# Two meetings of sequences in an attention and LoRA kernel: turns, router and value stores placed one or two products later, one scaling ahead of a score round

## The chip, the cores and the metric

The kernel runs on one core of a Trainium2 chip. The metric is the device time of one execution in microseconds (us). The time before is the median of three runs; a profile of one further execution is read beside it.

## The reference

Four sequences of 1024 rows with 1024 columns, all in float32. With x of shape (4, 1024, 1024):

```python
x = x + attn(layernorm(x), wq, wk, wv, wo)      # 32 heads of 32, rotary q and k, causal softmax
n = layernorm(x)
logits = n @ route_w.T                          # 8 experts
gate = one_hot(argmax(logits)) * max(logits)    # top 1
h = n @ A                                       # 8 experts x 16 hidden values
x = x + ((gate * h) @ Bw)
```

The layer norms have no weights. All weights of the attention are 1024 x 1024; the last step is a LoRA adapter of rank 16 for each of the 8 experts.

## The kernel before, in words

**Units and slots.** The kernel goes through 32 units: 4 sequences (b) of 8 head groups (g), each of 4 heads. Unit u has b = u // 8 and g = u % 8. A unit is a list of eleven slots (`SLOTS`). Nine are score rounds (`score_round`): the scores of one to four of the sixteen 64-row tiles go to PSUM, ScalarE (ACT) copies them to SBUF (L441), GpSimd (POOL) adds the causal mask on the diagonal (L444), VectorE (DVE) finds the row maxima, here called tops (L462, L483), ACT exponentiates in place (L491), and DVE turns the probabilities (L516). The two others, "second" and "first", apply the values (`apply`, L632): "second" those of the upper half of the unit before, "first" those of the lower half of this unit.

**What fills the slots.** Beside each unit stands a list of steps, `between[u]`: the q, k and v products of the next unit (`chain`, L337; eight 128x512 products for each of six chains), and from the second sequence on the end of the layer for one row tile of the sequence before (`finish_steps`): sixteen products of `wo` (`project`, L749, called `p` in the change; the first eight give the first half of the columns), then the tail: `turn` (transposes, L201, tensors pt_f), `route` (L771, ph), `turn_hidden` (L800, pw) and `adapt` (L810, pf, with the additions at L813 and the store of y at L814). The loop at the end of the function takes so many of these steps after each round. So the order of the instructions is written out by this Python code; each engine then works through its own list in order and waits on semaphores.

**The meeting of two sequences.** In the last unit of a sequence (g = 7) the products of the next unit need the next sequence, normalized and turned. `Norm` has these steps for each of eight row tiles of 128 rows: `load` (a DMA), `find` (mean and variance on DVE, L178 to L182, and the root on POOL, L184), `scale` (L189 on DVE), `turn` (eight transposes on TensorE, L201, tensors pt_a, then two copies by ACT to xnT, L203 and L205; then the next load). `change_steps` puts them in order among the last v chain of the present sequence (`h`, eight products held back for this), the wo products `p`, the tail, and the new chains. The first meeting (into b = 1) takes another branch. The second (u = 15) and the third (u = 23) take the branch `if p`, which the change rewrites. The lists `h`, `p` and `chains` are indexed in it, and the Python order in it is TensorE's order; a score round of the unit falls between two of its steps wherever the slot ends.

**Buffers.** A pool `ps` of four PSUM banks serves products, transposes and the tail; a new user waits until the engine that empties the old one is done. Chunks of wo, of the router weights (in_ra) and of the adapter (in_bw) go through four SBUF buffers (`take_chunk`, `load_chunk`): the load of chunk n + 4 is issued behind the product that used chunk n. In a meeting, tiles 3 and 6 of the new sequence lie in the next unit's qT, tile 4 in its kT.

**SyncE's queue.** All DMAs are issued by SyncE (SP), in the program's order. `stores` holds what is to be put to DRAM: the attention result of "second" (L665) and the unit's values (L531, four DMAs); they are issued in the loop at a slot given by `r`. The values are read back in another layout by eight DMAs (`loads`, L537), which `scatter` mixes into the steps to come, two apart. `second` is the index 2 in `SLOTS`; index 3 is the round of tiles 2, 1, 0 and 9, index 4 that of tile 15, index 5 that of tile 14.

Of the kernel before, what the change touches and what calls it, by code (L numbers as in the profile page):

```python
# [57 lines left out]
def weave(main, other):  # L58

    if not other:  # L60
        return list(main)
    out, taken = [], 0
    for n, step in enumerate(main):
        out.append(step)
        due = (n + 1) * len(other) // len(main)
        out += other[taken:due]
        taken = due
    return out + list(other[taken:])
# [3 lines left out]
def tile_preln_attn_then_top1_lora(  # L72
# [18 lines left out]
    B, S, D = x.shape  # L91
# [5 lines left out]
    NG = HEADS // HG  # L97
# [77 lines left out]
    def find_moments(src, name):  # L175
        stats = small.tile([P, D // 512, nc.vector.BN_STATS_DIM], F32, tag="stats", name=f"st_{name}")
        for i in range(D // 512):
            nc.vector.bn_stats(stats[:, i, :], src[:, i * 512 : (i + 1) * 512])  # L178
        mv = small.tile([P, nc.vector.BN_AGGR_DIM], F32, tag="mv", name=f"mv_{name}", bufs=3)
        nc.vector.bn_aggr(mv, stats)  # L180
        ve = small.tile([P, 1], F32, tag="ve", name=f"ve_{name}")
        nc.vector.tensor_scalar(ve, mv[:, 1:2], EPS, None, ALU.add)  # L182
        rstd = small.tile([P, 1], F32, tag="rstd", name=f"rstd_{name}", bufs=3)
        nc.gpsimd.tensor_tensor(rstd, ve, half_sb, ALU.pow)  # L184
        return mv, rstd
# [43 lines left out]
    def do_postponed(cost):  # L229
        for item in list(postponed):  # L230
            item[0] -= cost
            if item[0] <= 0:
                postponed.remove(item)
                item[1]()
# [12 lines left out]
    class Norm:  # L247
# [32 lines left out]
        def find(self, t):  # L280
            while self.found <= t and self.found in self.x:
                k = self.found
                self.moments[k] = find_moments(self.x[k], f"a{self.b}_{k}")
                self.found += 1
# [26 lines left out]
        def scaling(self, t):  # L311
            return Step(lambda: self.scale(t), 0.0)

        def turning(self, t):
            return Step(lambda: self.turn(t), 2.0 if self.b == 0 else 1.3)
# [169 lines left out]
    def release_exps():  # L485
        to_exp.extend(next_exp)
        next_exp.clear()
# [187 lines left out]
    def load_wo():  # L675

        for n in range(2):
            cols = slice(n * 512, (n + 1) * 512)
            wt = big.tile([P, NC, 512], F32, tag="xnT", name=f"wo_{n}", bufs=2)
            wo_all.append(wt)  # L680
            for c in range(NC):
                nc.sync.dma_start(wt[:, c, :], wo[c * P : (c + 1) * P, cols])
# [3 lines left out]
    def load_adapter():  # L686

        ra_all = NC * (E + ER)
        room = big.tile([P, ra_all + D + TB * D], F32, tag="prob0", name="adapter")
        kept["ra"] = room[:, :ra_all].rearrange("p (c n) -> p c n", n=E + ER)  # L690
        kept["bw"] = room[:ER, ra_all : ra_all + D]
        for k in range(TB):
            kept[k] = room[:, ra_all + D + k * D : ra_all + D + (k + 1) * D]
        nc.sync.dma_start(kept["ra"], ra.rearrange("(c p) n -> p c n", p=P))
        nc.sync.dma_start(kept["bw"], bw)
# [152 lines left out]
    def change_steps(u, norm, project, tail, held):  # L848

        p, h, turning, scaling = project, held, norm.turning, norm.scaling
        out, chains = [], []
        for n, tb in (("q", 0), ("k", 0), ("q", 1), ("k", 1), ("v", 0), ("v", 1)):
            chains += chain(u, n, tb)
        if p:
            turn, route, turn_hidden, adapt = tail
            find = norm.finding
            load_last = Step(lambda: norm.load(7), 0.0)
            out += [*h[:2], turn, *h[2:4], find(3), p[0], h[4], turning(2), h[5], p[1], route, scaling(3)]  # L860
            out += [find(4), h[6], p[2], h[7], p[3], turn_hidden, scaling(4), *p[4:6], adapt, load_last]
            out += [p[6], find(5), p[7], turning(3), scaling(5), *p[8:10], turning(4), *p[10:12]]
            chains = weave(chains[:-6], p[12:]) + chains[-6:]
            out += [*chains[:2], find(6), *chains[2:4], scaling(6), turning(5), *chains[4:6], find(7)]
            out += [*chains[6:8], scaling(7), turning(6), *chains[8:14], turning(7)]
            return out + chains[14:]
        for t, n in zip(range(TB, NT), (3, 4, 4, 4)):
            out += [*chains[:n], turning(t)]
            del chains[:n]
        return out + chains  # L870
# [149 lines left out]
    def do(s):  # L1020
        if s.chunk:
            s.run(numbers[s])
        else:
            s.run()
        do_postponed(s.cost)
# [40 lines left out]
    def scatter(steps, apart):  # L1066

        for k, s in enumerate(steps):
            todo.insert(min(len(todo), 1 + apart * k), s)

    n_slots = len(SLOTS)
    second, first_ = SLOTS.index("second"), SLOTS.index("first")
    final = len(units) - 1
    for u, (b, g) in enumerate(units):
        do_postponed(math.inf)
        do_postponed(math.inf)
        todo.extend(between[u])
        ends_at = n_slots
        if b + 1 < B and g + 1 == NG:
            if b:  # L1080
                norms[b + 1].load(3, 4)
        if u == final:
            load_wo()
            ends_at = second
        for r, pieces in enumerate(SLOTS):
            if pieces == "second":
                release_exps()
            if pieces == "second":
                if u == final:
                    todo.extend(early)  # L1090
                    ends_at = second + 3
                put, loads = spread_values(u)

                def meanwhile():
                    nc.vector.transpose(vTs[u], vTs[u])
                    if u in ahead_of:
                        ahead_of[u][0]()

                if u:
                    apply(u - 1, 1, meanwhile)  # L1100
                else:
                    meanwhile()
                stores.append(put)
            elif pieces == "first":
                apply(u, 0)
                find_tops(u)
                ended.clear()
            else:
                release_exps()
                turn_probabilities()  # L1110
                if second < r < first_:
                    join_sums(u, 0)
                if r == second + 1 and u in ahead_of:
                    ahead_of[u][1]()
                score_round(u, pieces)
                if r == second - 1 and u:
                    while any((u - 1, t) in places for t in range(QT, 2 * QT)):
                        exponentiate_some(1)
                        turn_probabilities()
                    join_sums(u - 1, 1)  # L1120
                if r != first_ - 1:
                    find_tops(u)
                exponentiate_some(SHARE / 3)
                next_exp.extend((u, t, h) for t in ended for h in range(HG))
                if r != first_ - 1:
                    ended.clear()
                if r in (second + 1, first_ + 1):
                    for put in stores:
                        put()
                    stores.clear()  # L1130
                    if u == final and r == first_ + 1:
                        load_adapter()
                if r == second + 2:
                    scatter(loads, 2)
                    if u in late_fetch:
                        do(late_fetch[u])
                        for k in range(3 if b == 1 else 0):
                            load_chunk(k)
            if u == final:
                if r == second + 3:  # L1140
                    todo.extend(parts)
                    ends_at = first_ + 2
                if r == first_ + 1:
                    todo.extend(wholes)
                    ends_at = n_slots + 2
            held_back = APART_BY if r < second else 0
            ahead = LENGTHS if not b and u + 1 < NG else [1.0] * ends_at
            fill(
                ahead[r] / sum(ahead[r:ends_at]),
                held_back,  # L1150
                0.0 if pieces in ("first", "second") else SHARE * 2 / 3,
            )
# [61 lines left out]
```

## Time and profile before

| | |
|---|---|
| median of 3 runs | 2727.84 us (2725.76 to 2735.31) |
| profiled execution | 2729.0 us, its span 2727.2 us |
| granted TensorE clock, mean | 0.995 |
| TensorE (PE) busy | 2671.2 us, 98% |
| VectorE (DVE) busy | 2141.2 us, 79% |
| ScalarE (ACT) busy | 1725.2 us, 63% |
| GpSimd (POOL) busy | 604.4 us, 22% |
| second meeting, about | 1150 to 1250 us from the span's start |
| third meeting, about | 1820 to 1920 us |

PEld is TensorE's load of the stationary operand, which overlaps its products. A wait is written as the waiting engine, tile and line, an arrow, and the engine, tile and line that ended it; then the total in us, how often, and the longest. A row of the timeline has the start, the duration, the engine, the line, the operation, the tile written and those read, and in brackets the idle time ahead of it. A float32 product stands as x2 in the timeline. Times are from the start of the span.

### The profile page before, as it was taken

To read this page: it belongs to the slowest core of one execution; us is meant where nothing else is said; L and a number is where in the kernel's file an instruction comes from. 1 tells how busy PE (TensorE), PEld (TensorE's weight loads), DVE (VectorE), ACT (ScalarE), POOL (GpSimd) and SP (SyncE) were. 2 spreads that over 40 slices of the span, in tenths; PEclk is the share of its full clock that TensorE was granted. 3 is DMA by queue.
4 is the path that set the end of the run, shared out by engine and by line. 5 is a ranking of instruction groups with operands and counts; after the bars stand their busy time and mean duration, and the time that the engine had idled before them with its cause. 6 is when DMAs were issued, how large, how long until landed. Compare 5 with 4: busy or idle time off the path is not lost.

```text
span 2727.2 us, 84063 instructions
## 1 busy us (share of the span) xinstructions
PE 2671.2 (98%) x35116; PEld 1305.0 (48%) x35116; DVE 2141.2 (79%) x4254; ACT 1725.2 (63%) x4980; POOL 604.4 (22%) x847
## 2 busy tenths in 40 slices
PE   8999999999999999989999999999999999999998
PEld 5444444444444544445444444444544444544445
DVE  4899999887777787887777878888778777777555
ACT  2878777876665676655666666766567666666421
POOL 2222222222221222222222222222212222222000
PEclk9999999999999999999999999999999999999999
DMA  3223233226555445652654444465354554446421
GB/s 118 60 72 74 75 77 84 53 56 174 139 140 131 126 131 155 167 157 61 163 161 134 135 131 132 136 187 142 83 159 135 159 136 133 131 132 185 123 69 53
DMA packets 465259, 332.19 MB, mean 122 GB/s; under 512 B 160496, under 2 KB 381936, under 8 KB 464880
## 3 DMA queue, kind: packets, MB, share of 16 engines
q1 hardware_dynamic: 464880, 326.83, 43.7%
q8 instruction: 276, 4.52, 0.7%
q14 instruction: 103, 0.84, 0.1%
HBM read 276.48 MB, written 50.24 MB: 120 GB/s over the span
## 4 chain that ended last, share of the span: by engine, by line
PE 79%; DVE 13%; ACT 3%; DMA 2%; POOL 1%; issue 1%; SPq 0%; POOLq 0%; DVEq 0%; ACTq 0%
PE po L749 15%; PE pq L337 14%; PE pk L337 13%; PE pv L337 11%; PE s L430 11%; PE av L632 8%; DVE top L462 4%; DVE pr L516 3%; PE ph L771 2%; PE pf L810 2%; ACT pr L491 1%; ACT pr L441 1%; DVE both L483 1%; PE pt_f L201 1%; DMA chunk<-in_wo 1%
## 5 line engine op out<-in xcount | busy, mean ns | idle before, releaser
L491 ACT ACTIVATE pr<-pr,both 128x256 f32<-128x256 f32 (+15 forms) x2048 | 1044.5, 519 | 55.5 <-DVE both L483 55.5
L441 ACT COPY pr<-s 128x640 f32<-128x640 f32 (+14 forms) x544 | 525.3, 1017 | 668.6 <-PE s L430 668.0
L462 DVE TENSOR_REDUCE top<-pr 128x2 f32<-128x960 f32 (+15 forms) x768 | 650.6, 893 | 256.8 <-POOL pr L444 256.2
L516 DVE STREAM_TRANSPOSE pr<-pr 128x1024 f32<-128x1024 f32 (+11 forms) x768 | 664.5, 907 | 33.7 <-ACT pr L491 30.4
L444 POOL TENSOR_TENSOR pr<-pr,causal_sb 128x128 f32<-128x128 f32 x512 | 239.0, 473 | 1152.2 <-ACT pr L441 1143.9
L337 PE MATMUL pv<-xnT,wv 128*128 128x512 f32 x1024 | 486.2, 602 | 0.0
L337 PE MATMUL pq<-xnT,wq 128*128 128x512 f32 x1008 | 479.1, 603 | 0.2 <-ACT xnT L203 0.2
L337 PE MATMUL pk<-xnT,wk 128*128 128x512 f32 x1008 | 476.8, 602 | 0.0
L430 PE MATMUL s<-kT,qT 32*32 32x256 f32 (+4 forms) x17408 | 393.8, 385 | 8.7 <-POOL pr L444 3.3
L491 ACT ACTIVATION_READ_ACCUMULATOR pr<-pr,both 128x1 f32 x2048 | 401.3, 196 | 0.0
L749 PE MATMUL po<-chunk,attn 128*128 128x512 f32 x736 | 379.7, 601 | 4.8 <-DMA chunk<-in_wo 4.8
L430 PEld LDWEIGHTS s<-kT,qT 32*32 32x32 f32 x17408 | 187.5, 103 | 266.2 <-issue 100.8
L337 PEld LDWEIGHTS pk<-xnT,wk 128*128 128x128 f32 x1008 | 181.2, 190 | 234.8 <-issue 234.5
L337 PEld LDWEIGHTS pq<-xnT,wq 128*128 128x128 f32 x1008 | 183.8, 192 | 226.1 <-issue 224.2
L337 PEld LDWEIGHTS pv<-xnT,wv 128*128 128x128 f32 x1024 | 185.6, 190 | 218.0 <-issue 217.2
L632 PE MATMUL av<-pr,vals 64*32 64x256 f32 (+3 forms) x12288 | 273.6, 321 | 6.9 <-DVE pr L516 6.5
L632 PEld LDWEIGHTS av<-pr,vals 64*32 64x32 f32 x12288 | 214.9, 106 | 115.5 <-issue 69.8
L483 DVE TENSOR_TENSOR both<-top 32x4 f32<-32x4 f32 (+3 forms) x1152 | 206.6, 179 | 23.8
L749 PEld LDWEIGHTS po<-chunk,attn 128*128 128x128 f32 x736 | 135.2, 190 | 170.1 <-issue 147.5
L652 DVE TENSOR_TENSOR at<-av,by 128x256 f32<-128x256 f32 x128 | 48.1, 417 | 110.0 <-PE av L632 71.5
L749 PE MATMUL po<-wo,attn 128*128 128x512 f32 x256 | 119.1, 607 | 2.3 <-DMA attn<-attn 2.3
L370 POOL TENSOR_TENSOR qT<-rawq,cos_sb 128x512 f32<-128x512 f32 x64 | 82.1, 1283 | 143.0 <-ACT rawq L363 143.0
(89 smaller groups left out, 1565.9 us busy)
## 6 DMA issues: line engine op xcount, KB each, us to landing
chunk<-in_wo SPq DMA_DIRECT2D x368, 256.0 KB, 3.8
vals<-vd SPq DMA_DIRECT2D x256, 128.0 KB, 4.3
x<-in_x SPq DMA_DIRECT2D x56, 512.0 KB, 5.0
wq<-in_wq SPq DMA_DIRECT2D x32, 512.0 KB, 4.7
wk<-in_wk SPq DMA_DIRECT2D x32, 512.0 KB, 3.9
wv<-in_wv SPq DMA_DIRECT2D x32, 512.0 KB, 4.2
vd<-vT SPq DMA_DIRECT2D x128, 128.0 KB, 4.5
out_y<-x SPq DMA_DIRECT2D x32, 512.0 KB, 2.6
```

Source lines behind the costliest of these rows:

```text
L337: nc.tensor.matmul(at["p"], lhsT=wt[:, c, :], rhs=xnTs[b, tb][:, c, :], start=(c == 0), stop=(c == NC - 1),)
L370: nc.gpsimd.tensor_tensor(dst[:, cols], raw, cos_sb[:, cols], ALU.mult)
L430: nc.tensor.matmul(sc[i * SQ : (i + 1) * SQ, h, at : at + w].rearrange("p (j k) -> p j k", k=SQ), lhsT=of_q[rows, 2 * t + half], rhs=of_k[ ...
L441: nc.scalar.copy(pr[:, :, k0 : k0 + w], sc[:, :, at : at + w])
L444: nc.gpsimd.tensor_tensor(diagonal, diagonal, causal_sb.unsqueeze(1).to_broadcast([P, HG, SQ]), ALU.add)
L462: nc.vector.tensor_reduce(top[:, k, h : h + step], places[u, t][:, h : h + step, :], AX.X, ALU.max, negate=True,)
L483: nc.vector.tensor_tensor(dst[rows], src[rows], src[other], op)
L491: nc.scalar.activation(pr[:, h, :], pr[:, h, :], AF.Exp, bias=tops[u, t][:, h : h + 1], accum_out=dens[u, t // QT][:, t % QT, h : h + 1],)
L516: nc.vector.transpose(pr, pr)
L632: nc.tensor.matmul(avs[half][h * HD : (h + 1) * HD, t0:, :], lhsT=v[rows, j, h * HD : (h + 1) * HD], rhs=rhs, start=(j == 0), stop=(j == n ...
L749: nc.tensor.matmul(st["po"], lhsT=lhsT, rhs=rhs, start=(c == start), stop=(c == stop))
L771: nc.tensor.matmul(ph, lhsT=st["ynT"][:, c, :], rhs=w[:, c - i * RA, :], start=(c == 0), stop=(c == NC - 1),)
```

## The change

Three things change, for the second and third meeting alone.

1. In `change_steps` tile 2's turn, the router, tile 3's turn and tile 4's turn stand one or two products later among the v products `h` and the wo products `p`; `p[3]` and `p[4]` both stand ahead of `turn_hidden`.
2. Tile 6 (the seventh) is scaled one chain product earlier, which puts it ahead of the score round that falls there; its turn stays where it was.
3. In the loop, the stores of the attention result and of the values are issued one slot later (after the round of tile 15 in place of that of tile 2), and the loads of the values are scattered one slot later too.

```diff
-            out += [*h[:2], turn, *h[2:4], find(3), p[0], h[4], turning(2), h[5], p[1], route, scaling(3)]
-            out += [find(4), h[6], p[2], h[7], p[3], turn_hidden, scaling(4), *p[4:6], adapt, load_last]
-            out += [p[6], find(5), p[7], turning(3), scaling(5), *p[8:10], turning(4), *p[10:12]]
+            out += [*h[:2], turn, *h[2:4], find(3), p[0], h[4], p[1], h[5], turning(2), h[6], p[2], route]
+            out += [scaling(3), find(4), h[7], p[3], p[4], turn_hidden, scaling(4), p[5], adapt, load_last]
+            out += [p[6], find(5), p[7], p[8], turning(3), scaling(5), p[9], p[10], turning(4), p[11]]
             chains = weave(chains[:-6], p[12:]) + chains[-6:]
-            out += [*chains[:2], find(6), *chains[2:4], scaling(6), turning(5), *chains[4:6], find(7)]
-            out += [*chains[6:8], scaling(7), turning(6), *chains[8:14], turning(7)]
+            out += [*chains[:2], find(6), chains[2], scaling(6), chains[3], turning(5), *chains[4:6]]
+            out += [find(7), *chains[6:8], scaling(7), turning(6), *chains[8:14], turning(7)]
             return out + chains[14:]
...
-                if r in (second + 1, first_ + 1):
+
+                meet = b and b + 1 < B and g + 1 == NG
+                if r in (second + (2 if meet else 1), first_ + 1):
                     for put in stores:
                         put()
                     stores.clear()
                     if u == final and r == first_ + 1:
                         load_adapter()
+                if r == second + (3 if meet else 2):
+                    scatter(loads, 2)
                 if r == second + 2:
-                    scatter(loads, 2)
                     if u in late_fetch:
                         do(late_fetch[u])
```

## The prediction

> **What bounds the kernel now.** I read the page first: TensorE (PE) is busy for 98% of the span, so only time in which PE waits, or runs at a lowered clock, can be won back.
>
> ```profile
> span 2727.2 us, 84063 instructions
> PE 2671.2 (98%) x35116; PEld 1305.0 (48%) x35116; DVE 2141.2 (79%) x4254; ACT 1725.2 (63%) x4980; POOL 604.4 (22%) x847
> ```
>
> The busy time by stage shows where. Columns: stretch, its length, PE, PEld, DVE, ACT and POOL busy, granted clock, DMA share, GB/s.
>
> ```profile
> 1150.00:1250.00 100.00, 92.11 (x1129) 46.19 (x1133) 79.33 (x161) 59.98 (x169) 23.57 (x34) 0.98 0.48 137
> 1250.00:1820.00 570.00, 569.51 (x7597) 274.19 (x7596) 451.53 (x900) 368.79 (x1073) 127.13 (x176) 1.00 0.51 139
> 1820.00:1920.00 100.00, 92.95 (x1193) 47.52 (x1184) 81.82 (x163) 61.63 (x171) 23.62 (x34) 1.00 0.50 141
> 1920.00:2500.00 580.00, 580.00 (x7706) 279.02 (x7689) 458.05 (x909) 372.49 (x1082) 129.11 (x177) 1.00 0.49 135
> ```
>
> The two changed meetings idle PE for 7.9 and 7.1 us. Between and after them PE is full, so what a meeting gains or loses reaches the end one to one. The waits of PE in the second meeting:
>
> ```profile
> PE po L749 <- DMA chunk<-in_wo: 2.3, 2, 1.3
> PE pt_a L201 <- DVE qT L189: 2.3, 1, 2.3
> PE pt_a L201 <- ACT yn L203: 2.1, 1, 2.1
> PE pt_a L201 <- ACT xnT L203: 0.7, 1, 0.7
> PE pw L800 <- DVE wh L790: 0.5, 1, 0.5
> ```
>
> They are, in time: tile 2's turn (2.12), the turned hidden row (0.51), tile 3's turn (0.68), two chunks of wo (1.31 and 0.98), tile 6's turn (2.26). The third meeting repeats them 672.4 us later, with one chunk wait of 1.47. Each has a row of the change aimed at it. The question is what is late next.
>
> **First clue: VectorE (DVE).** From 1147 to 1196 it is busy 46.57 of 49 us, in both meetings, and the chain of waits runs along it from 1140 to 1183 almost without a break.
>
> ```profile
> 1147.00:1196.00 49.00, 45.66 (x767) 25.18 (x782) 46.57 (x94) 30.84 (x87) 9.27 (x16) 1.00 0.53 161
> ```
>
> The order of the built kernels shows DVE's own order unchanged up to tile 6's scaling. POOL's order does not change at all. So PE can run ahead there, but its next wait on DVE comes at the same time as before.
>
> **Part 1, tile 2's turn and the router.** PE's new order after the product at 1165.34 is: product of wo, scores of tile 5, v product, turn, v product, wo, router (ph), v product, values (av). With the old steps (0.86 a product, 0.95 before scores, 1.57 for these scores, 0.96 after them, 0.93 a turn) the turn comes at 1169.7, behind ACT's two copies of yn (ended 1168.92): the 2.12 is gone. But the router's bank is the one the turn filled, and ACT must empty it.
>
> ```profile
> 1168.33 0.59 ACT L205 COPY yn<-pt_f 128x512 f32<-128x512 f32 x1
> 1170.43 0.58 ACT L203 COPY xnT<-pt_a 128x512 f32<-128x512 f32 x1
> 1171.37 1.89 ACT L441 COPY pr<-s 128x768 f32<-128x768 f32 x3
> ```
>
> On ACT that copy now stands behind the scores' copies (1.75), two exponentials of 288 (1.05) and two of 256 (1.0): 1170.43 + 3.8 + 0.57 = 1174.8. PE arrives at 1172.5, so a new wait of 2.34 takes the old one's place. Router 1.86 and product 0.96 lead to av at 1177.65; av needs DVE's four transposes of probabilities, ended 1177.75 before and not earlier now. Before, av started at 1177.77. Gain: 0.1.
>
> **Part 2, the hidden row.** One more product stands ahead of pw, so wh (DVE, 1182.97) is waited for no longer: gain 0.5, and with smaller steps the second half of av starts at 1184.24 instead of 1185.01.
>
> **Part 3, tile 3's turn.** The first product of the second half of wo moves ahead of it, and now takes the bank of the spread sums. The turn gets the banks of pf, which DVE empties with the two additions at L813 (ended 1193.18). DVE had one gap here, 0.35 for ACT's copy of the sums, which comes 0.77 earlier: so 1192.83. The chunk of the moved product is issued after pf and took 2.9 to land: PE waits 0.45 for it and twice, 0.3 and 0.6, for L813. Scores of tile 2 start at 1194.37 instead of 1194.80: gain 0.43.
>
> **Part 4, tile 4's turn and the chunks.** SP's queue (start, length):
>
> ```profile
> 1193.21 0.34 SPq L814 DMA_DIRECT2D out_y<-x  x1
> 1193.61 0.42 SPq L126 DMA_DIRECT2D x<-in_x  x1
> 1194.14 1.27 SPq L706 DMA_DIRECT2D chunk<-in_wo x2
> ```
>
> The two awaited chunks stand behind the store of y, which waits for L813. They move by L813's 0.35 only: landing near 1198.69 instead of 1199.04, the second near 1200.8. The attention and value stores, moved a slot on, stood behind them already; in 1197 to 1201 only 62 packets were under 512 B. Taking them away gives between nothing and 0.9 (the attention store's 256 KB at the 281 GB/s of 1195 to 1205); I take nothing, as the landings follow the order of issue. One of the chunks is now wanted ahead of tile 4's turn, which covered 0.93 of its landing: PE arrives at 1196.28 and waits 2.41 (2.55 in the third meeting, where the landing was 0.16 later), then turns, then takes the second chunk, which has landed by then. In the third meeting this order alone loses 0.6, as its second chunk was never late.
>
> **The clock.** Idle PE costs a second time:
>
> ```profile
> 1197.00:1207.00 10.00, 7.71 (x19) 3.25 (x17) 5.59 (x14) 4.30 (x14) 2.29 (x5) 0.83 0.90 246
> 2556.00:2566.00 10.00, 7.67 (x34) 3.15 (x14) 4.87 (x13) 4.90 (x16) 0.45 (x1) 0.83 0.96 211
> 1210.00:1220.00 10.00, 7.74 (x54) 3.37 (x53) 8.03 (x15) 8.09 (x28) 2.25 (x3) 1.00 0.47 96
> ```
>
> 0.83 over 10 us is 1.7 us lost (8 products at 1203.01 took 4.25 against 3.60). In PE's timeline single waits of 2.33, 2.40, 2.60, 2.70 and 3.91 were all followed by it, one of 2.23 was, and those of 2.12, 2.13, 2.26 and 2.27 were not; the two chunk waits, 2.29 together, were. The Trainium skill ("TensorE: Matmul & The Clock Gate", on how the gate oscillates in real kernels) asks only that PE not idle for over some 3.4 us. By that rule no new wait here lowers the clock, and the second meeting even sheds its 1.7. By the rows, 2.41 and 2.55 both lower it. I take the rows: second meeting 1.7 as before, third meeting 1.7 new. The router's 2.34 is at the edge; I take it as not.
>
> **Part 5, tile 6 scaled ahead of a round.** DVE was idle for 6.2 us ahead of the tops of tile 15, and the scaling stood behind them. The tile's load now stands behind one more chunk and lands about 0.5 later (1203); with 1.65 of statistics, 0.55 on POOL and 0.8 the scaling ends near 1206.2, before the turn's 1212.2 and before the tops are due (1209.5). The 2.26 goes. Next late is ACT: the first k product needs the bank of rawq, whose copy ends 7.07 after the start of the scores of tile 15, 0.6 after PE arrives.
>
> **Part 6, stores and loads of values.** The attention and value stores (7.85 of SP's time before) stand behind the last two wo chunks. Six of eight value loads now also stand behind a router chunk, whose buffer comes free at about 1217. They land near 1217.5 + 2.9 + 4.1 = 1224.5; av of this unit starts near 1237. Cost nothing, with 12 us of cover.
>
> **The sum.** Second meeting: scores of tile 15 start at 1198.69 + 0.86 (chunk) + 0.93 (turn) + 0.86 (chunk) + 3.57 (four q products) + 1.7 (clock) = 1206.6; first k product at 1206.6 + 7.07 = 1213.7, before 1215.95: gain 2.25. Third, in the second's times: 1206.8, and 1213.87 against 1213.46: loss 0.4. Together 1.85. The profiled execution took 2729.0 (2727.2 and 1.8 around the span), so 2727.15; the median of the runs is 1.16 lower: 2726.0.
>
> **Rivals.**
> - *No new half clock* (the skill's rule): for it, the nearest wait of 2.27 passed at full clock; against it, five of five from 2.33 on. The gains are then 3.7 and 1.3: 2722.8. Chance 0.25.
> - *The router's wait lowers the clock too*: av, the sums and L813 come later, by 1.1 net a meeting: 2728.2 for both. It shares 0.65 with my forecast.
> - *The waits vanish as aimed at*: 7.9 + 7.1 + 1.7 = 16.6, so 2711. Against it: DVE's full 49 us. Chance 0.03.
> - *Slower: the values come late.* SP's queue is in order, and six value loads now wait behind a chunk's release. Each microsecond by which they land after av is due shows once in each meeting. It decides from 1237, 12.5 us later than I reckon; 0.5% slower (13.6 us) needs 1245.5, giving 2743. For it, the stores took 8.0 to land in a crowded queue; against it, the queue is empty by then. Chance 0.05.
>
> About 0.5% is what a measurement of this kernel can tell from no change; nothing but the last two passes it, and 0.02 is left for what I overlook. Range 2721 to 2731: 1.8 below the second case and 2.8 above the third, for the scatter of runs (2725.8 to 2735.3). Chances: faster 0.03, same 0.91, slower 0.06.
>
> **What would show it.** Right: PE's waits list ph behind ACT xnT (2.3, twice), po behind a chunk (2.4 to 2.6, twice), pt_a behind DVE x (under 1), and none on yn or qT; half-clock stretches in both meetings near 1199 and 1871. Wrong: a chunk wait under 1.5 (the landing moved with PE), av before 1177, or any wait of av on vals.

## The result, and the profile after

| | before | after |
|---|---|---|
| median of 17 runs, us | 2729.38 (2724.47 to 2737.35) | 2724.51 (2720.74 to 2729.37) |
| ratio, 95% interval | | 0.9984 [0.9977, 0.9991] |

The change makes the kernel 4.9 us faster by the medians, 2.5 to 6.3 by the interval. That is less than 0.5% and more than the 1.85 us of the forecast; the median lies inside its range, between the forecast (2726.0) and the rival without new half clock (2722.8). The profiled execution after took 2727.9 (its span 2726.1), more than the median of its runs, so its span alone tells little. First lines of its page:

```profile
span 2726.1 us, 84061 instructions
PE 2670.2 (98%) x35116; PEld 1305.3 (48%) x35116; DVE 2141.5 (79%) x4254; ACT 1725.0 (63%) x4980; POOL 602.5 (22%) x847
```

Nothing there shows a gain of 0.2%. The busy time by stage, after (stretch, length, PE, PEld, DVE, ACT, POOL busy, granted clock, DMA share, GB/s):

```profile
1150.00:1250.00 100.00, 94.53 (x1195) 48.58 (x1184) 81.53 (x163) 61.68 (x171) 23.36 (x34) 0.98 0.49 142
1250.00:1820.00 570.00, 568.27 (x7563) 273.52 (x7547) 450.29 (x898) 367.20 (x1070) 126.76 (x176) 1.00 0.51 139
1820.00:1920.00 100.00, 94.87 (x1155) 48.06 (x1154) 80.58 (x159) 63.30 (x173) 23.27 (x34) 0.97 0.48 138
1920.00:2500.00 580.00, 580.00 (x7677) 279.07 (x7676) 458.85 (x910) 371.57 (x1080) 128.85 (x178) 1.00 0.49 136
```

The meetings now idle TensorE for 5.5 and 5.1 us, where it was 7.9 and 7.1. But the clock of the third fell to 0.97: a busier TensorE there is partly a slower one. Its waits, in the second meeting and then in the third:

```profile
PE po L749 <- DMA chunk<-in_wo: 2.5, 1, 2.5
PE ph L771 <- ACT xnT L203: 2.1, 1, 2.1
PE pk L337 <- ACT rawq L363: 0.6, 1, 0.6
```

```profile
PE po L749 <- DMA chunk<-in_wo: 2.5, 2, 2.3
PE ph L771 <- ACT xnT L203: 2.0, 1, 2.0
PE pk L337 <- ACT rawq L363: 0.6, 1, 0.6
```

The waits on yn, on wh, on xnT ahead of tile 3 and on tile 6's qT, at which the change aimed, are gone. Two of the three in their place are as long as the old ones: the router's and the chunk's. TensorE's timeline has them with their times; first two rows of the second meeting, then two of the third:

```profile
1176.85 3.58 PE L771 MATMUL ph<-chunk,yn 128*128 128x136 f32 x16 [2.07 <-ACT xnT L203]
...
1202.01 1.12 PE L749 MATMUL po<-chunk,attn 128*128 128x512 f32 x2 [2.49 <-DMA chunk<-in_wo]
```

```profile
1848.33 2.67 PE L771 MATMUL ph<-chunk,yn 128*128 128x136 f32 x16 [1.99 <-ACT xnT L203]
...
1873.21 1.69 PE L749 MATMUL po<-chunk,attn 128*128 128x512 f32 x2 [2.27 <-DMA chunk<-in_wo]
```

A router of 3.58 us, against 2.02 before, and a pair of products of 1.69 against 1.12 ran at half clock, wholly or in part; the pair behind 2.49, the longest wait, did not. This contradicts any rule by the length of the wait alone.

To compare meetings I take the stretch from the start of the turn of yn (pt_f) to the start of the first k product, the same instructions in both kernels:

| | second meeting | third meeting |
|---|---|---|
| before | 54.06, one half clock | 51.57, none |
| after | 51.50, one half clock | 52.44, two half clocks |

At a full 1.7 us for each half clock (at most that: part of it can lie beside a wait), the waits themselves gave 2.6 us in the second meeting and up to 2.5 us in the third.

### The profile page after: what moved, and what is told of

Read it like the earlier page. It is cut to its first block, busy times and chain, and to the rows that moved or that the text cites. A ratio compares the mean times of both kernels' runs of the same rounds, so it can differ in the third digit from the quotient of the medians.

```text
span 2726.1 us, 84061 instructions
## 1 busy us (share of the span) xinstructions
PE 2670.2 (98%) x35116; PEld 1305.3 (48%) x35116; DVE 2141.5 (79%) x4254; ACT 1725.0 (63%) x4980; POOL 602.5 (22%) x847
## 4 chain that ended last, share of the span: by engine, by line
PE 79%; DVE 12%; ACT 3%; DMA 2%; issue 1%; POOL 1%; SPq 1%; POOLq 0%; DVEq 0%; ACTq 0%
PE po L749 14%; PE pq L337 14%; PE pk L337 13%; PE pv L337 12%; PE s L430 11%; PE av L632 9%; DVE top L462 3%; DVE pr L516 3%; PE ph L771 2%; PE pf L810 2%; ACT pr L491 2%; DMA chunk<-in_wo 1%; ACT pr L441 1%; DVE both L483 1%; PE pt_f L201 1%
## 5 line engine op out<-in xcount | busy, mean ns | idle before, releaser
L652 DVE TENSOR_TENSOR at<-av,by 128x256 f32<-128x256 f32 x128 | 48.2, 418 | 112.0 <-PE av L632 72.8
```

## The experiments

Each kernel was timed in five rounds beside the kernel before on the same chip, whose median was 2728.2, 2727.9 and 2728.6 us in the three groups (e1 to e4, e5 to e8, e9 to e12). Ratios are to that kernel, each with its 95% interval. There were 16, 13, 21 and 21 runs of e1 to e4, 5, 10, 13 and 5 of e5 to e8, and 22, 22, 6 and 6 of e9 to e12: e5, e8, e11 and e12 are the least sure.

### The scaling of tile 6 alone (e1), and everything but it (e2)

e1 against the kernel before; e2 is the kernel after with these two lines as before.

```diff
-            out += [*chains[:2], find(6), *chains[2:4], scaling(6), turning(5), *chains[4:6], find(7)]
-            out += [*chains[6:8], scaling(7), turning(6), *chains[8:14], turning(7)]
+            out += [*chains[:2], find(6), chains[2], scaling(6), chains[3], turning(5), *chains[4:6]]
+            out += [find(7), *chains[6:8], scaling(7), turning(6), *chains[8:14], turning(7)]
```

e1: 

> The kernel before with one of the three edits: the scaling of tile 6 stands one chain product earlier; turns, router and value stores as before. Theory (the scaling carries the gain, the turns and the router only move their waits): TensorE's wait of 2.26 us ahead of the seventh tile's transposes goes in both meetings, and 0.6 us for rawq comes ahead of the first k product, so 1.7 us off each meeting, 3.3 us off the whole, some 2726 us by the median before of 2729.4 and a ratio of about 0.9988; nothing else in the meetings moves. Rival (turns and router bring the gain): the wait ahead of the seventh tile goes, but the first k product starts no earlier, and the time stays within 1 us of before.

e2: 

> The kernel after without the scaling edit: turns, router and value stores moved, the scaling of tile 6 back behind the fourth chain product. Theory: TensorE's waits for the router's copy (2.0) and for the chunk of w_o (2.3 to 2.5) stay as in the kernel after, the 2.26 us ahead of tile 6 come back in both meetings, so about 3.3 us slower than after and within 1.5 us of before, some 2728 us. Rival (turns and router bring the gain): 4 to 5 us below before, as after.

Measured: e1 2723.58 us, ratio 0.9981 [0.9973, 0.9988]; e2 2729.00 us, ratio 1.0000 [0.9992, 1.0009]. The scaling alone brings the whole gain; the rest of the change brings nothing that these runs can tell (e2's interval is 2 us and more to each side). TensorE's waits of e1 in the second meeting (timeline):

```profile
1169.37 1.14 PE L201 MATMUL pt_a<-eye_sb,x 128*128 128x128 f32 x8 [2.12 <-ACT yn L203]
...
1193.91 0.66 PE L201 MATMUL pt_a<-eye_sb,qT 128*128 128x128 f32 x4 [0.68 <-ACT xnT L203]
...
1200.62 1.13 PE L749 MATMUL po<-chunk,attn 128*128 128x512 f32 x2 [1.47 <-DMA chunk<-in_wo]
...
1202.72 1.12 PE L749 MATMUL po<-chunk,attn 128*128 128x512 f32 x2 [0.98 <-DMA chunk<-in_wo]
...
1214.33 1.12 PE L337 MATMUL pk<-xnT,wk 128*128 128x512 f32 x2 [0.64 <-ACT rawq L363]
```

The 2.26 ahead of tile 6 is gone, and 0.64 of it came back at the first k product, so 1.6 us went in each meeting. VectorE's timeline shows how, first before, then e1: the scaling (L189 on qT) stands ahead of the tops of tile 15, in time that was idle.

```profile
1210.95 2.35 DVE L462 TENSOR_REDUCE top<-pr 128x2 f32<-128x1024 f32 x2 [6.20 <-POOL pr L444]
...
1214.09 0.81 DVE L189 TENSOR_SCALAR qT<-qT,mv_a,rstd_a 128x1024 f32<-128x1024 f32 x1
```

```profile
1206.43 0.81 DVE L189 TENSOR_SCALAR qT<-qT,mv_a,rstd_a 128x1024 f32<-128x1024 f32 x1 [0.73 <-POOL rstd_a L184]
...
1210.97 2.35 DVE L462 TENSOR_REDUCE top<-pr 128x2 f32<-128x1024 f32 x2 [3.11 <-POOL pr L444]
```

The other old waits are there, except the 0.51 for wh, which is missing here, where a half clock behind the first wait made TensorE late, and stands in the third meeting. And e2, second meeting:

```profile
1174.13 2.12 PE L771 MATMUL ph<-chunk,yn 128*128 128x136 f32 x16 [2.20 <-ACT xnT L203]
...
1197.81 1.13 PE L749 MATMUL po<-chunk,attn 128*128 128x512 f32 x2 [2.37 <-DMA chunk<-in_wo]
...
1212.27 1.06 PE L201 MATMUL pt_a<-eye_sb,qT 128*128 128x128 f32 x8 [2.26 <-DVE qT L189]
```

It has the waits of the kernel after for the router and the chunk, and the old one for tile 6. The forecast of some 2726 us was too high: twice 1.6 us is 3.2, and e1's gain is 4.6 us by the medians and 5.2 by the ratio (3.3 to 7.4). The 3.2 lies just below the interval. What is beyond the waits fits fewer half clocks: the mean granted clock was 0.9967 over its 16 runs, 0.9957 over the 60 of before beside it.

### Value stores back in their old slot (e3)

The kernel after with the third part of the change undone.

```diff
-                if r in (second + (2 if meet else 1), first_ + 1):
+                if r in (second + 1, first_ + 1):
...
-                if r == second + (3 if meet else 2):
-                    scatter(loads, 2)
                 if r == second + 2:
+                    scatter(loads, 2)
```

> The kernel after with the value stores and their loads put back to where they were in rounds before the change. Theory: the stores' place is worth nothing, 2724.5 us, within 1 us of after; the stores again stand between the chunks in SP's queue but land long ahead of need. Rival (the stores moved off SP's queue let the chunks of w_o leave earlier): the wait for the chunk in the meetings grows from 2.3 to 2.5 by 0.5 us or more each, and the time by 1 to 3 us.

Measured: 2724.38 us, ratio 0.9984 [0.9977, 0.9990], the same as the kernel after. The stores' place is worth nothing that these runs can tell. Its one profile has a chunk wait of 4.07 us in the second meeting, as the rival forecast, but 2.41 in the third; the median shows no sign of the former. From issue to product that chunk took 6.5 us, against 4.9 in the third meeting, where the queue had the same order, so the order alone is not its cause, which stays open.

### Tile 4's turn back ahead of a product (e4)

```diff
-            out += [p[6], find(5), p[7], p[8], turning(3), scaling(5), p[9], p[10], turning(4), p[11]]
+            out += [p[6], find(5), p[7], p[8], turning(3), scaling(5), p[9], turning(4), p[10], p[11]]
```

> The kernel after with the turn of tile 4 ahead of the eleventh product of the output projection again, its place before the change. Theory (the chunks of w_o stand in SP's queue behind the store of y, and land when they did before; only the work that covers their landing was moved): the wait for the chunk falls from 2.3 to 2.5 us to about 1.5 us, so 0.9 us less in each meeting, and with one or two stretches of half clock fewer 2720 to 2723 us. Rival (the turn of tile 4 needs VectorE's scaling that early, so the wait moves to the turn): the sum of waits between the eighth product and the turn stays at 2.3 to 2.5 us in each meeting and the time at 2724.5 us.

Measured: 2723.42 us, ratio 0.9980 [0.9973, 0.9987]: not told apart from the kernel after. The longest wait did fall as I expected, but a second came behind it. Second meeting, timeline:

```profile
1202.85 1.12 PE L749 MATMUL po<-chunk,attn 128*128 128x512 f32 x2 [1.68 <-DMA chunk<-in_wo]
1204.94 2.07 PE L749 MATMUL po<-chunk,attn 128*128 128x512 f32 x2 [0.97 <-DMA chunk<-in_wo]
```

With the 0.16 of the chunk ahead of tile 3's turn these are 2.8 us, no less than the 2.5 of the kernel after (2.3 in the third meeting). The forecast of 2720 to 2723 us and of fewer half clocks missed: its profile has two in each meeting. The rival's result held, though not by its wait: the two chunks land at times of their own, and it is the second that is waited for when the turn no longer stands between the two. The pair took 2.07 us: half clock again, though neither wait ahead of it reached 1.7.

### The store of y behind the chunks (e5), and the turn of tile 2 one step back (e7, e8)

If the chunks are late because SP's queue holds them behind the store of tile 6's y, which waits for VectorE's L813, the store has to move. (This y is row tile 6 of the sequence that ends, not the tile 6 of the new one, which is scaled.) e5 is the kernel after with:

```diff
-            nc.sync.dma_start(out[b, t * P : (t + 1) * P, :], y)
+            put = lambda: nc.sync.dma_start(out[b, t * P : (t + 1) * P, :], y)
+            late_out.append(put) if t == 6 and b < 2 else put()
...
-            load_last = Step(lambda: norm.load(7), 0.0)
+            load_last, put_y = Step(lambda: norm.load(7), 0.0), Step(lambda: late_out.pop()(), 0.0)
...
-            out += [p[6], find(5), p[7], p[8], turning(3), scaling(5), p[9], p[10], turning(4), p[11]]
+            out += [p[6], find(5), p[7], p[8], turning(3), scaling(5), p[9], put_y, p[10], turning(4), p[11]]
```

> The kernel after, with the store of tile 6's y in the second and third meeting put into SP's queue behind the chunks and inputs that stood behind it (after the tenth product of the output projection). Theory (the chunk of w_o waits in SP's queue behind that store, which itself waits for VectorE's L813): the chunks are issued some 3.5 us earlier, TensorE's wait for the chunk of 2.3 to 2.5 us falls below 0.5 us in both meetings, 4 to 5 us, and with it the half clock that follows about two of three such waits (1.7 us each), some 2 us more: 2717 to 2720 us against 2724.5 of after. Rival (the chunk's landing is set by the transfer itself, or TensorE runs into VectorE's queue behind it at the next turn): the chunk's wait shrinks, but the seventh tile's transposes or the first k product wait by as much more, and the time stays within 1.5 us of after.

Measured: 2715.97 us, ratio 0.9962 [0.9949, 0.9974], a little below the forecast. SP's queue of the kernel after, then of e5 (start, time in the queue):

```profile
1196.13 0.34 SPq L814 DMA_DIRECT2D out_y<-x  x1
1196.53 0.42 SPq L126 DMA_DIRECT2D x<-in_x  x1
1197.06 1.74 SPq L706 DMA_DIRECT2D chunk<-in_wo  x3
```

```profile
1190.25 0.42 SPq L126 DMA_DIRECT2D x<-in_x  x1
1190.77 2.35 SPq L706 DMA_DIRECT2D chunk<-in_wo  x3
...
1195.33 0.44 SPq L814 DMA_DIRECT2D out_y<-x  x1
```

The chunks are issued 6.3 us earlier by the clock of the span, 3.5 us earlier against the meeting's own work (the products of pf started at 1190.71 after, at 1187.96 in e5). TensorE's waits of e5 in the second meeting:

```profile
PE ph L771 <- ACT xnT L203: 2.1, 1, 2.1
PE pk L337 <- ACT rawq L363: 0.6, 1, 0.6
PE po L749 <- DMA chunk<-in_wo: 0.4, 1, 0.4
```

The chunk's wait is 0.4 us (0.3 in the third meeting), and nothing behind it grew: pk still waits 0.6. From the turn of yn to the first k product it took 49.11 and 46.95 us, with one half clock in the former. The cause of the chunk's wait is shown: the store ahead of it in the queue.

e7 is the kernel after, and e8 is e5, each with:

```diff
-            out += [*h[:2], turn, *h[2:4], find(3), p[0], h[4], p[1], h[5], turning(2), h[6], p[2], route]
+            out += [*h[:2], turn, *h[2:4], find(3), p[0], h[4], p[1], turning(2), h[5], h[6], p[2], route]
```

e7: 

> The kernel after with the turn of tile 2 between the second product of the output projection and the sixth held product, one step less far moved. The copies of tile 2's transposes then stand ahead of one exponential of 0.5 us on ScalarE, so the router's wait falls from 2.0 to 2.4 us to some 1.5 to 1.9 us. Theory on the clock (a stretch of half clock of 3.4 us follows a window of the same length in which TensorE was idle for about 1.8 us or more, wherever the wait comes from): no half clock after the router in either meeting, 0.5 us of wait and in the mean 0.9 us of half clock less per meeting, 2721 to 2723 us. Rival (the half clock follows any wait of 1.5 us or more, or is not tied to the waits): half clock at the router in at least one meeting, 2724 us.

e8: 

> The kernel after with both: the store of tile 6's y behind the chunks and the turn of tile 2 one step earlier. Theory: the gains add, since the router's wait and the chunk's wait lie one behind the other on TensorE: no wait above 1.9 us and no half clock in the second and third meeting, 2714 to 2718 us. Rival (both only move one wait that VectorE's queue sets): not below the late store alone by more than 0.5 us.

Measured: e7 2724.30 us, ratio 0.9986 [0.9977, 0.9994]; e8 2715.46 us, ratio 0.9959 [0.9946, 0.9971], not told apart from e5. e7's forecast of 2721 to 2723 us missed, and so did that of no half clock at the router: the second meeting has one. e8's 2714 to 2718 was met, but so was its rival (e8 is 0.5 us below e5). e7's second meeting shows where the half microsecond went:

```profile
1172.39 3.67 PE L771 MATMUL ph<-chunk,yn 128*128 128x136 f32 x16 [1.92 <-ACT xnT L203]
1197.88 1.12 PE L749 MATMUL po<-chunk,attn 128*128 128x512 f32 x2 [2.83 <-DMA chunk<-in_wo]
```

The router waits 1.92 (1.33 in the third meeting), less than the 2.07 and 1.99 of after, but the chunk's wait is longer: what TensorE gains ahead of it is lost there. In e8, where no chunk is late, the router waited 1.56 and 1.93 and neither meeting had a half clock, as forecast; the time still did not fall by more than these runs can tell.

### Each edit with the late store (e6, e9 to e12)

These complete the table of three edits: the turns and router (with the value stores), the scaling, the late store. e9 is the kernel before with the late store; e10 is e2 with it; e6 and e11 are e1 with it, one kernel in two groups; e12 is e5 again. The lines are those of e5; in e6, e9 and e11 the store stands at the same place of the old order:

```diff
-            out += [p[6], find(5), p[7], turning(3), scaling(5), *p[8:10], turning(4), *p[10:12]]
+            out += [p[6], find(5), p[7], turning(3), scaling(5), *p[8:10], put_y, turning(4), *p[10:12]]
```

e6: 

> The kernel before with the scaling of tile 6 one chain product earlier and the store of tile 6's y behind the chunks: turns, router and value stores stand where they stood before the change. Theory: the chunk's waits of 1.3 to 2.5 us per meeting go, 3 to 4 us off the 2723.6 us of the scaling alone, some 2720 us; what is left is the wait of 2.1 us ahead of tile 2's turn with its half clock. Rival (with the chunk out of the way, the moved turns and router pay): this kernel stays 2 us or more above the kernel after with the same late store.

e9: 

> The kernel before with the late store of tile 6's y as the only edit: scaling of tile 6, turns, router and value stores as before. Theory A (each edit takes its own wait, and the turns and the router only hand theirs on): the chunk's waits of 1.3 to 2.3 us per meeting go, some 3 to 4 us, about 2724 us; the seventh tile's wait of 2.26 us stays. Rival (the late store only pays once the scaling has been moved, since TensorE runs into the seventh tile's wait behind it): the seventh tile's wait grows to 3.5 us or more, the time within 1 us of before.

e10: 

> Turns, router and value stores moved as in the kernel after, with the late store of y, but the scaling of tile 6 in its old place. Theory A (turns and router are worth nothing): within 1 us of the kernel before with the late store alone. Theory B (what the turns and the router save was lost again at the chunk, and is kept once the chunk comes in time): 1.5 to 3 us below the kernel before with the late store alone, since the waits of 2.1 ahead of the turn, 0.5 for wh and 0.7 for the second half of tile 3 become one of about 2 us for the router.

e11: 

> The scaling of tile 6 and the late store of y on the kernel before, once more, on the same chip as the kernel with all edits. Theory A: within 1 us of that one. Theory B: 1.5 to 3 us above it.

e12: 

> The kernel after with the late store of y, once more. Both theories: 2714 to 2718 us, and 7 us or more below the kernel after. Theory A: within 1 us of the kernel without the moved turns and router. Theory B: 1.5 to 3 us below it.

Measured, ratio to the kernel before:

| | turns and router as before | turns and router moved |
|---|---|---|
| neither | 1 | 1.0000 [0.9992, 1.0009] (e2) |
| scaling | 0.9981 [0.9973, 0.9988] (e1) | 0.9984 [0.9977, 0.9991] (after) |
| late store | 0.9975 [0.9969, 0.9982] (e9) | 0.9977 [0.9971, 0.9983] (e10) |
| both | 0.9971 [0.9962, 0.9980] (e6), 0.9967 [0.9954, 0.9979] (e11) | 0.9962 [0.9949, 0.9974] (e5), 0.9964 [0.9951, 0.9977] (e12) |

Read across, the turns and the router are worth nothing that the runs can tell: the differences are 0.0000, +0.0003, +0.0002 and -0.0006, well inside the intervals. After e6 I had thought that they pay once the chunk comes in time, as e6 came out 3.6 us above e5, as its rival forecast; run again, e11 (2718.59) and e12 (2717.27) are only 1.3 us apart, between the two theories, and e9 and e10 (2722.73 and 2722.36) 0.4. In the last row, with 11 and 16 runs, up to some 3 us are not excluded.

The traces say what the times cannot. In meetings without a half clock, from the turn of yn to the first k product, e6 and e11 took 48.03 to 48.05 us and e5 46.95 (e8, with tile 2's turn a step back, 47.13 and 47.53); e9 took 49.67 and e10 49.13. So with the chunk in time the turns and the router save some 0.5 to 1.1 us a meeting; without the late store they save nothing (51.57 in the third meeting of before, 51.79 in the second of e2). But a half clock stood behind the moved router in four of the six meetings of e5, e10 and e12, and behind the old wait on yn in two of the six of e6, e9 and e11. These are few meetings; that the one takes back the other is my reading, not shown.

The e9 rival is refuted: 2.26 and 2.27 us, the seventh tile's wait did not grow. Down the columns, the late store is worth 0.0010 to 0.0025 and the scaling 0.0004 to 0.0019. The fastest versions, e5 and e8, are 10 to 11 us below before by their ratios and 6 to 7 below after, e5's second group (e12) 9.8 and 5.5; their ratios do not tell them apart.

## Why the prediction was right or wrong

**Parts 1 and 2, turn and router.** Right: 2.34 was forecast for the router on xnT, 1.99 to 2.07 came (2.20 and 2.37 in e2). One wait took the place of another, and no worth of the edit can be told from the times of e2 and the table. Wrong only in the clock.

**Part 3, tile 3's turn.** Too pessimistic: I had 0.45 for its chunk and twice 0.3 to 0.6 for L813. After shows 0.24 for the chunk in the third meeting and nothing else; e2, whose second meeting ran at full clock, 0.17 and 0.28. Two things differ from the forecast. In e2 L813 ended 30.65 us after the start of the turn of yn, against 31.29 before: 0.64 earlier, where I had 0.35. In after TensorE itself came late, by the half clock at the router, and VectorE with it. VectorE's gap ahead of L652, which I had taken to close, was 1.27; before, then after:

```profile
1188.64 0.76 DVE L652 TENSOR_TENSOR at<-av,by 128x256 f32<-128x256 f32 x2 [0.35 <-ACT by L604]
1191.57 0.76 DVE L652 TENSOR_TENSOR at<-av,by 128x256 f32<-128x256 f32 x2 [1.27 <-ACT by L604]
```

L813 then ended 31.88 and 31.74 after the start of the turn, 1.1 to 1.2 later than in e2, and with it came the store of y and the chunks behind it. The other profiles agree: in the nine with the moved turns (after, e2 to e5, e7, e8, e10, e12) L813 ended 30.2 to 30.9 after that start in the eight meetings without a half clock at the router, and 31.6 to 32.2 in the ten with one. For the sum the waits of this part matter little: what TensorE does not wait here it waits for the chunk, whose landing follows L813.

**Part 4, the chunks.** Right in size: 2.41 and 2.55 forecast; 2.49 and 2.27 came, and 2.37 in e2's meeting at full clock. The half clock at the router, which the forecast did not have, changed this wait little, as it moved TensorE and L813 alike. Right in cause: e5 takes the wait away by moving the store of y and nothing else.

**Part 5, the scaling.** Right: the 2.26 goes, 0.6 for rawq was forecast, 0.64 came in both meetings, and no wait of DVE's took its place. By e1 and e2 this is the whole of the gain that can be told.

**Part 6, values.** Right: e3 is equal, and no wait of av on vals appears.

**The clock.** The step that failed, though the total stayed inside its range. The forecast counted one new half clock in the third meeting, by the length of the wait, and none for the router. In the profile of after the router had one in both meetings, and the chunk of 2.49 none; of the two stretches named as signs, near 1199 and 1871, only the latter came. A sum with fixed costs by the length of a wait could not come out; the right term is a chance. By the mean clock of the runs, after (0.9956 in 17) and before (0.9957 in the 60 beside e1 to e4) have about alike many half clocks, so the net term was near 0 where I put 1.7. Waits alone made 3.55 us in my sum (2.25 and 1.3); the waits listed above fall by 2.7 and 1.9, 4.6 together, and the stretches give up to 5.1. With no net clock all three lie inside the 2.5 to 6.3 of the interval. So 1.7 of the 3.0 that the forecast lacked is the clock; the rest, in the waits, is no more than the noise of the runs.

**The rivals.** "No new half clock" named the right total (5.0 of gain), though not for its reason: new half clocks came, and by the mean clock about as many old ones went. "The router's wait lowers the clock too" named the right place, and its 1.1 us of delay for L813 is what came in both meetings (1.1 to 1.2); its sum was wrong, since it kept the half clocks at both chunks as well. That all waits vanish, or that the values come late, is excluded by the waits shown.

## What to carry to other kernels

Where TensorE waited on engines that were full, moving its work changed mostly which instruction waited: the router's 2.1 us for the turn's 2.1. Look for the edit whose releaser had idle time before it (VectorE's 6.2 us ahead of the tops of tile 15), and for an in-order queue in which a load stands behind a store that waits. Here the order of one DMA was worth at least as much as the whole change (0.0025 in e9, 0.0016 in after; their intervals overlap). And small differences need many runs on one chip: a difference of 3.6 us between two kernels was 1.3 when they were run again.

## What the hardware showed

Half clock goes by a fixed grid of time, not by the length of a wait. In the traces' record of the granted clock, every change lies on a grid of 3.413 us that runs on through the whole execution, and its phase against the span's start differs between executions: the first half-clock stretch began at 135.9 us before, 135.1 in e7 and 134.1 in e5. Laid out by this grid, TensorE's busy time and the clock in the kernel after:

```profile
1173.91:1177.32 3.41, 1.34 (x7) 1.00 0.72 222
1177.32:1180.73 3.41, 3.41 (x16) 0.50 0.34 96
...
1197.80:1201.21 3.41, 1.72 (x128) 1.00 0.99 282
1201.21:1204.63 3.42, 2.51 (x11) 1.00 1.02 381
...
1870.23:1873.64 3.41, 1.14 (x33) 1.00 0.93 320
1873.64:1877.06 3.42, 3.42 (x11) 0.50 0.88 326
```

and in the kernel before:

```profile
1166.77:1170.18 3.41, 1.70 (x47) 1.00 0.13 36
1170.18:1173.59 3.41, 3.41 (x74) 1.00 0.50 159
1197.49:1200.90 3.41, 1.37 (x5) 1.00 1.01 317
1200.90:1204.31 3.41, 3.17 (x4) 0.50 1.05 289
```

(Columns: stretch, length, TensorE busy, granted clock, DMA share, GB/s.) A window with 1.34, 1.14 or 1.37 us of work (2.0 to 2.3 idle) is followed by one at 0.50. The wait of 2.49 fell across a boundary, 1.69 and 0.80, and was not; nor was before's 2.12, 1.71 of it in one window. Before's two chunk waits of 1.31 and 0.98, and e4's of 1.68 and 0.97, were, since most of both lay in one window.

The same sum over the fourteen profiles (this one, the one before, e1 to e12), for all windows of the clock's record, which begins 11 to 16 us into the span, that were themselves at full clock; idle is the time without a matmul in the profile:

| TensorE idle in the window, us | windows | followed by half clock |
|---|---|---|
| under 1.55 | 10888 | 0 |
| 1.55 to 1.85 | 38 | 5 |
| 1.85 to 2.03 | 11 | 7 |
| 2.03 and more | 64 | 64 |

So the bound is near 1.9 us, a little over half a window. The Trainium skill's rule, which the prediction weighed ("TensorE: Matmul & The Clock Gate", on how the gate oscillates: no idle gap over about 3.4 us), has the length of the window but not the condition: 2.03 us of idle inside one was enough each time, and several short waits add up. A wait of 2.3 us that meets the grid at a random phase has, as an estimate from a bound of 1.9, a chance of (3.4 - 1.9 + 2.3 - 1.9) / 3.4, about 0.56, of costing up to 1.7 us more; one under 1.9 alone has none. Each stretch lowers the mean clock of a run by 0.0006. In the 60 runs of the kernel before beside e1 to e4, the seven at 0.994 had a mean span of 2729.4 us and the fourteen at 0.997 one of 2724.9: part of the scatter from run to run is the number of these stretches. A straight line through the 60 clocks and spans accounts for about a third of the variance; the rest is open.
